# Five of the 47 expert tiles move from the main pipeline into a conditional block at the end of the program

## The chip, the cores and the metric

The kernel runs on one core of one Trainium2 chip. The metric is device microseconds of one execution. Beside it there is one profiled execution, with a trace of every engine: PE (matrix multiply; its weight loads are listed apart as PEld), DVE (vector), ACT (scalar activation), POOL (general purpose) and SP (issues most transfers).

## The reference, cut to what matters

Two layers on x of shape (4, 512, 256), all in float32. Layer 0 adds a linear attention with a running sum and a top-32 "gene" block. Layer 1 adds a running-sum mixer with a gated feed-forward part, and a mixture of experts:

```
xn = layernorm(x)                                  # 2048 tokens of 256
scores = softmax(xn @ gate_w.T)                    # 16 experts
topk_w, topk_idx = top_k(scores, 2)
gu = einsum('th,ehj->etj', xn, w_gate_up)          # 256 -> 352, per expert
h  = silu(gu[..., :176]) * gu[..., 176:]
y  = einsum('eti,eih,te->th', h, w_down, combine)  # only the two chosen experts count
y += swiglu(xn @ shared_gate_up) @ shared_down
```

Each token goes to two of 16 experts, which makes 2048 · 2 = 4096 rows of experts' work. How they are spread over the experts depends on the data.

## The kernel before, in words

**Main phases.** Tokens are worked on in 16 blocks of 128 (`NTT`). First layer 0 (`layer0`) and the layer-1 mixer (`mix`) run batch by batch, with the dense part of layer 1 (`dense`: shared expert and gated feed-forward, 88 steps of one chunk each) woven in between as filler for PE. `together` weaves generators by their weights.

**Routing.** `route` (L460 to L539) counts the tokens of each expert, rounds each count up to tiles of 128 rows and sums them up: `upto` holds the running number of tiles, so that its last element is the number of tiles that the routing needs. `offs` holds, for each of the `NTL` = 47 tiles, the offset of its expert's weights; 47 is the most that 4096 rows over 16 experts can need (32 full tiles and 15 more that are begun). `slot` and `cpair` give, for each token and choice, its row and its weight.

**Rows by way of DRAM.** `xrows` and `yrows` are arrays of 47 · 128 rows of 256 in DRAM. Early in the program one transfer (L173) fills `xrows` with zeros. `scatter` (L541) writes each token's row twice to `xrows` with 32 indirect transfers from POOL's queue, again beside dense steps. L682 to L793 are the experts' stage. It works in pairs of tiles: `fetch` (L707) loads two tiles of `xrows`; `turn_in` (L714) transposes them on PE, copies them to SBUF on ACT, and loads the pair's two offsets into PE registers; `up_tile` (L735) multiplies by the expert's gate and up weights, in the SBUF tile `wex` that holds all 16 experts, and makes silu on ACT and the product on DVE; `turn_hidden` (L751) transposes again; `down_pair` (L756) multiplies by the down weights, and the result goes to `yrows` on SP's queue. 47 tiles are 23 pairs and a single one, and `experts` (L774) runs 26 steps in which three pairs are in flight.

**The end.** Behind the experts come the last dense steps, with 32 indirect gathers (L806, `ys` from `yrows`, POOL's queue), 32 weighted adds on DVE (L817) and the stores of the output (L821, L826). The whole of `yrows` has to be written before the first gather starts.

**Order.** The order on each engine follows from the order in which the program issues its steps and from a scheduler that sets independent instructions among each other; on each engine the instructions then run in order. Transfers marked `paced` wait for the last dense matmul issued before them.

Of the kernel before, what the change touches and what calls it, by code (L numbers as in the profile page):

```python
# [11 lines left out]
F32 = mybir.dt.float32  # L12
AF = mybir.ActivationFunctionType
ALU = mybir.AluOpType
AX = mybir.AxisListType

P = 128
B, L, D = 4, 512, 256
NT = L // P
NH = D // P  # L20
# [3 lines left out]
NE, NI = 16, 176  # L24
EI = NE * NI
SI = 2 * NI
EW = NH * 2 * NI + 2 * D
NTT = B * NT
NTL = 47
XG = 2  # L30
HB = 2 * P
QSCALE = 0.25
# [5 lines left out]
def run_all(steps):  # L38
    for _ in steps:
        pass  # L40


def together(*streams):

    live = [[iter(steps), n, 0] for steps, n in streams]
    while live:
        s = min(live, key=lambda s: s[2] / s[1])
        s[2] += 1
        if next(s[0], live) is live:
            live.remove(s)  # L50
# [3 lines left out]
def tile_two_layers(  # L54
# [23 lines left out]
    nc = tc.nc  # L78
    V, S, G, T = nc.vector, nc.scalar, nc.gpsimd, nc.tensor

    const = ctx.enter_context(tc.tile_pool(name="const", bufs=1))


    xs = const.tile([P, B, NT, D], F32, name="xs")
# [7 lines left out]
    def paced(inst):  # L92

        tc.add_manual_dep(
            inst,
            beat[-1],
            mybir.DependencyInfo(mybir.DependencyClass.Sync, mybir.DependencyReason.DATA),
            reason="transfers spread over the dense parts",
        )
        return inst  # L100
# [61 lines left out]
    cpair = const.tile([P, 2, NTT], F32, name="cpair")  # L162
    slot = const.tile([P, 2, NTT], mybir.dt.int32, name="slot")
    offs = const.tile([1, NTL], mybir.dt.int32, name="offs")
    chosen = const.tile([P, NTT, NE], F32, name="chosen")
    cwall = const.tile([P, NTT, NE], F32, name="cwall")
    xn1 = const.tile([P, B, NT, D], F32, name="xn1")
# [1 line left out]
    yrows = tc.dram_tile([NTL * P, D], F32, name="yrows")  # L169
    zero = wp.tile([P, D], F32, name="zero")  # L170
    G.memset(zero, 0.0)

    nc.sync.dma_start(  # L173
        xrows.rearrange("(j p) d -> p j d", p=P), zero[:, None, :].to_broadcast([P, NTL, D])
# [285 lines left out]
    def route():  # L460


        rt = routing.enter_context(tc.tile_pool(name="rt", bufs=1))
        ps_r = routing.enter_context(tc.tile_pool(name="ps_r", bufs=1, space=bass.MemoryType.PSUM))

        stri = rt.tile([P, P], F32, name="stri")
        G.memset(stri, 1.0)
        G.affine_select(
            out=stri, in_=stri, pattern=[[1, P]], compare_op=ALU.is_gt, fill=0.0, base=0, channel_multiplier=-1
        )  # L470
        allone = rt.tile([P, P], F32, name="allone")
        G.memset(allone, 1.0)
        kfull = rt.tile([P, NE, NTT], F32, name="kfull")
        G.iota(
            kfull, pattern=[[0, NE], [P, NTT]], base=0, channel_multiplier=0, allow_small_or_imprecise_dtypes=True
        )
        jnum = rt.tile([P, NTL, NE], F32, name="jnum")
        G.iota(
            jnum, pattern=[[1, NTL], [0, NE]], base=0, channel_multiplier=0, allow_small_or_imprecise_dtypes=True
        )  # L480
        first0 = rt.tile([P, NE, NTT], F32, name="first0")
        G.memset(first0, 1.0)
        G.memset(first0[:, :, 0:1], 0.0)
        pr = ps_r.tile([P, L], F32, name="pr")
        flat = chosen.rearrange("p t e -> p (t e)")
        T.matmul(pr[:, 0 : NTT * NE], stri, flat, start=True, stop=True)
        T.matmul(pr[:, NTT * NE : L], allone, flat, start=True, stop=True)
        cnt = rt.tile([P, NE, NTT], F32, name="cnt")
        V.tensor_copy(cnt, pr[:, NTT * NE : L].rearrange("p (t e) -> p e t", e=NE))
        inc = rt.tile([P, NE, NTT], F32, name="inc")  # L490
        V.tensor_tensor_scan(
            inc.rearrange("p e t -> p (e t)"),
            first0.rearrange("p e t -> p (e t)"),
            cnt.rearrange("p e t -> p (e t)"),
            0.0,
            ALU.mult,
            ALU.add,
        )
        yield

        more = rt.tile([P, NE, NTT], F32, name="more")
        V.tensor_tensor(more, inc[:, :, NTT - 1 : NTT].to_broadcast([P, NE, NTT]), kfull, ALU.is_gt)
        nt = rt.tile([P, NE], F32, name="nt")
        V.tensor_reduce(nt, more, AX.X, ALU.add)
        upto = rt.tile([P, NE], F32, name="upto")
        V.tensor_tensor_scan(upto, allone[:, 0:NE], nt, 0.0, ALU.mult, ALU.add)
        yield

        past = rt.tile([P, NTL, NE], F32, name="past")
        V.tensor_tensor(past, upto[:, None, :].to_broadcast([P, NTL, NE]), jnum, ALU.is_le)  # L510
        ex = rt.tile([P, NTL], F32, name="ex")
        V.tensor_reduce(ex, past, AX.X, ALU.add)
        V.tensor_scalar(offs, ex[0:1], float(NE - 1), float(EW), ALU.min, ALU.mult)
        yield

        V.tensor_tensor(upto, upto, nt, ALU.subtract)
        V.tensor_scalar(upto, upto, float(P), 1.0, ALU.mult, ALU.add)
        V.tensor_tensor(inc, inc, cnt, ALU.subtract)
        V.tensor_tensor(inc, inc, upto[:, :, None].to_broadcast([P, NE, NTT]), ALU.add)
        row = rt.tile([P, NTT, NE], F32, name="row")  # L520
        V.tensor_tensor(
            row,
            pr[:, 0 : NTT * NE].rearrange("p (t e) -> p t e", e=NE),
            inc.rearrange("p e t -> p t e"),
            ALU.add,
        )
        V.tensor_tensor(row, row, chosen, ALU.mult)
        yield
        two = rt.tile([P, 2, NTT], F32, name="two")
        V.tensor_reduce(two[:, 0], row, AX.X, ALU.max)  # L530
        V.tensor_reduce(two[:, 1], row, AX.X, ALU.add)
        V.tensor_tensor(two[:, 1], two[:, 1], two[:, 0], ALU.subtract)
        V.tensor_scalar(slot, two, -1.0, None, ALU.add)
        for k in range(2):
            hit = rt.tile([P, NTT, NE], F32, name="hit")
            V.tensor_tensor(hit, row, two[:, k, :, None].to_broadcast([P, NTT, NE]), ALU.is_equal)
            V.tensor_tensor(hit, hit, cwall, ALU.mult)
            V.tensor_reduce(cpair[:, k], hit, AX.X, ALU.add)  # L538
        yield  # L539
# [23 lines left out]
    NC = len(chunks)  # L563
# [63 lines left out]
    def d(n):  # L627
        return islice(dd, n), n
# [4 lines left out]
    def m(b, i0, nt):  # L633
        return mix(b, i0, nt), 6 + nt
# [13 lines left out]
    weights = ctx.enter_context(ExitStack())  # L648
    we = weights.enter_context(tc.tile_pool(name="we", bufs=1, side="right"))


    wex = we.tile([P, NE * EW], F32, name="wex")
    wev = wex.rearrange("p (e w) -> p e w", w=EW)
    G.memset(wev[:, :, EW - D : EW], 0.0)

    def load_experts():
        wdv = w_down.rearrange("(e i) d -> i e d", i=NI)
        for e in range(0, NE, 4):
            es = slice(e, e + 4)
            for h in range(NH):  # L660
                paced(
                    nc.sync.dma_start(
                        wev[:, es, h * 2 * NI : (h + 1) * 2 * NI],
                        w_gate_up[es, h * P : (h + 1) * P, :].rearrange("e p j -> p e j"),
                    ).ins
                )
                yield
            paced(nc.sync.dma_start(wev[:, es, EW - 2 * D : EW - D], wdv[0:P, es]).ins)
            yield
            paced(nc.sync.dma_start(wev[0 : NI - P, es, EW - D : EW], wdv[P:NI, es]).ins)  # L670
            yield

    together(m(3, 0, 4), d(NC), (load_experts(), 17))
    mixing.close()
    routing = ctx.enter_context(ExitStack())
    together((route(), 8), d(5))
# [2 lines left out]

    run_all(islice(dd, 2 * NC - 19))  # L680

    wx = ctx.enter_context(tc.tile_pool(name="wx", bufs=2))  # L682
    hbs = []
    for k in range(2):
        hb = wx.tile([P, XG, 2 * P], F32, name=f"hb{k}", bufs=1)
# [2 lines left out]
    ps_u = ctx.enter_context(tc.tile_pool(name="ps_u", bufs=2, space=bass.MemoryType.PSUM))  # L688
    ps_x = ctx.enter_context(tc.tile_pool(name="ps_x", bufs=1, space=bass.MemoryType.PSUM))
    marks = []  # L690
    NP2 = (NTL + XG - 1) // XG
    pairs = {}

    def width(p):
        return min(XG, NTL - p * XG)

    def turned(src, m, name):

# [75 lines left out]
    def experts():  # L774

        for p in range(2):
            fetch(p)
        for s in range(NP2 + 2):
            if s + 2 < NP2:
                fetch(s + 2)  # L780
            if 0 <= s - 1 < NP2:
                up_tile(s - 1, 0)
            if s < NP2:
                turn_in(s)
            if 0 <= s - 1 < NP2:
                up_tile(s - 1, 1)
            if s - 2 >= 0:
                down_pair(s - 2)
            if 0 <= s - 1 < NP2:
                turn_hidden(s - 1)  # L790
            yield

    together((experts(), NP2 + 2))  # L793
    weights.close()

    back = ctx.enter_context(tc.tile_pool(name="back", bufs=1, side="right"))
    ys = back.tile([P, 2 * NTT, D], F32, name="ys")
    asked = 0  # L800
    added = 0
# [22 lines left out]
    assert asked == added == 2 * NTT  # L824
    for i in (NT - 2, NT - 1):
        nc.sync.dma_start(out[B - 1, i * P : (i + 1) * P], xs[:, B - 1, i])  # L826


# [47 lines left out]
```

## Time and profile before

| what | value |
|---|---|
| median of 3 runs | 586.94 us (586.6 to 588.18) |
| the profiled execution's own time | 591.42 us |
| its span in the trace | 589.7 us |
| mean granted PE clock | 0.975 |
| PE busy | 539.4 us (91%) |
| DVE, ACT, POOL busy | 373.1, 232.6, 173.9 us |
| the experts' stage, about 400 to 523 us | PE busy 122.04 of 123 us |

The span runs from the first to the last record of the trace; the execution's own time lies 1.7 us above it. The profiled execution took 4.5 us longer than the median of the runs. A row of the groups gives line, engine, operation, output and input tiles, count, then busy time and mean duration in ns, then the idle time ahead of them and what ended it. A row of the timeline begins with start and length in microseconds. One float32 matmul of the program appears as two passes in the trace, so a tile's two up matmuls are four rows.

### The profile page before, as it was taken

The numbers are of one execution on the slowest core, as the hardware profiler recorded it, in microseconds if no ns is written. First come the engines' busy times: TensorE is split into PE (matmuls) and PEld (weight loads), VectorE is DVE, ScalarE is ACT, GpSimd is POOL, SyncE is SP. The second block draws the span as 40 slices with busy tenths as digits, with TensorE's granted clock in tenths as the row PEclk, the third lists the DMA queues.
The fourth block names the chain that finished last, engine by engine and source line by source line (L and its number), as shares of the span: only waits on it lengthen the run. The fifth ranks groups of instructions, "written<-read, shape, count | busy, mean of one in ns | idle before, by whom it ended". The sixth has DMA issues, their size and how long they took to land.

```text
span 589.7 us, 7350 instructions
## 1 busy us (share of the span) xinstructions
PE 539.4 (91%) x2384; PEld 393.0 (67%) x2384; DVE 373.1 (63%) x992; ACT 232.6 (39%) x528; POOL 173.9 (29%) x214
## 2 busy tenths in 40 slices
PE   3557989989999999999999999969999999999987
PEld 1334656558565685656877778857777777788876
DVE  3979999997896797967943785322222222235563
ACT  1453746653555625556265311103333333321111
POOL 1234232353221432224440326661000000006651
PEclk9788999999999999999999999989999999999999
DMA  4993000000000000000075602224233333114441
GB/s 159 375 377 140 1 1 1 2 0 1 1 1 0 1 1 1 1 1 1 1 236 170 182 2 80 91 86 136 90 108 107 108 108 98 55 63 125 126 133 46
DMA packets 38453, 47.39 MB, mean 80 GB/s; under 512 B 4016, under 2 KB 34960, under 8 KB 38160
## 3 DMA queue, kind: packets, MB, share of 16 engines
q1 hardware_dynamic: 35344, 38.53, 20.0%
q0 software_dynamic: 3072, 8.39, 4.6%
q8 instruction: 20, 0.33, 0.2%
q14 instruction: 17, 0.14, 0.1%
HBM read 28.30 MB, written 18.61 MB: 80 GB/s over the span
## 4 chain that ended last, share of the span: by engine, by line
PE 61%; DVE 21%; ACT 6%; POOL 4%; issue 3%; DMA 2%; SPq 0%; another core or an unknown queue 0%; POOLq 0%; ACTq 0%; DVEq 0%
PE gu L576 16%; PE pu L740 9%; PE acc L596 9%; PE py L761 7%; PE pm L384 5%; DVE rep L302 4%; DVE top L301 4%; PE pt L703 3%; POOL xrows L544 3%; PE pm L244 3%; PE pm L289 2%; PE pm L221 2%; PE pm L339 2%; DVE sums L430 2%; DVE sums L421 1%
## 5 line engine op out<-in xcount | busy, mean ns | idle before, releaser
L576 PE MATMUL gu<-yT,wugt 128*128 128x256 f32 x512 | 127.5, 385 | 0.0
L576 PEld LDWEIGHTS gu<-yT,wugt 128*128 128x128 f32 x512 | 96.0, 192 | 19.5 <-issue 7.2
L580 ACT ACTIVATE th<-gu 128x256 f32<-128x256 f32 (+1 forms) x88 | 33.0, 382 | 133.4 <-PE gu L576 85.9
L806 POOL DMA_INDIRECT ys<-yrows,slot x32 | 30.7, 961 | 145.4 <-PE gu L576 130.1
L596 PE MATMUL acc<-wot,hid 128*128 128x256 f32 x256 | 67.4, 386 | 5.9 <-DVE hid L584 5.5
L582 DVE SCALAR_TENSOR_TENSOR th<-th,gu 128x256 f32<-128x256 f32 (+1 forms) x88 | 36.1, 412 | 55.0 <-ACT th L580 46.3
L740 PE MATMUL pu<-wex,xgT 128*128 x188 | 63.8, 461 | 0.8 <-DMA xg<-xrows 0.8
L587 POOL TENSOR_TENSOR hid<-hid,th 128x256 f32<-128x256 f32 (+1 forms) x44 | 34.3, 782 | 101.1 <-ACT hid L586 97.8
L596 PEld LDWEIGHTS acc<-wot,hid 128*128 128x128 f32 x256 | 48.4, 192 | 15.5 <-DVE hid L584 5.9
L244 PE MATMUL pm<-xnT,wqkv 128*128 128x512 f32 (+1 forms) x120 | 46.7, 529 | 4.1 <-ACT lg L293 1.8
L576 PE MATMUL gu<-xn1T,sgu 128*128 128x256 f32 (+1 forms) x192 | 47.3, 382 | 1.4 <-ACT hid L586 1.3
L749 DVE TENSOR_TENSOR hb<-pu,hb 128x176 f32<-128x176 f32 x47 | 16.1, 342 | 51.0 <-ACT hb L748 51.0
L384 PE MATMUL pm<-w,xn1T 128*128 128x512 f32 (+1 forms) x128 | 45.7, 501 | 0.0
L761 PE MATMUL py<-wex,hgT 128*128 x188 | 44.5, 379 | 0.0
L761 PEld LDWEIGHTS py<-wex,hgT 128*128 128x128 f32 x188 | 35.6, 190 | 8.6 <-issue 0.2
L576 PEld LDWEIGHTS gu<-xn1T,sgu 128*128 128x128 f32 (+1 forms) x192 | 33.8, 181 | 9.5 <-ACT hid L586 2.6
L740 PEld LDWEIGHTS pu<-wex,xgT 128*128 128x128 f32 x188 | 32.0, 190 | 11.0 <-ACT xgT L717 1.0
L384 PEld LDWEIGHTS pm<-w,xn1T 128*128 128x128 f32 x128 | 24.6, 193 | 21.4 <-issue 17.9
L244 PEld LDWEIGHTS pm<-xnT,wqkv 128*128 128x128 f32 x120 | 23.8, 202 | 22.0 <-issue 13.2
L753 DVE COPY hgT<-pt 128x512 f32<-128x512 f32 (+1 forms) x24 | 16.3, 681 | 34.2 <-PE pt L703 34.2
L544 POOL DMA_INDIRECT xrows<-xn,slot x32 | 31.0, 969 | 23.8 <-DVE cpair L538 9.9
L301 DVE MAX8 top<-rep 128x8 f32<-128x512 f32 x48 | 32.9, 686 | 0.4
(162 smaller groups left out, 881.5 us busy)
## 6 DMA issues: line engine op xcount, KB each, us to landing
xrows<-zero SPq DMA_DIRECT2D x1, 6016.0 KB, 22.6
xg<-xrows SPq DMA_DIRECT2D x23, 256.0 KB, 2.7
yrows<-yg SPq DMA_DIRECT2D x23, 256.0 KB, 2.1
wex<-in_w_gate_up_dram SPq DMA_DIRECT2D x8, 704.0 KB, 4.8
xs<-in_x_dram SPq DMA_DIRECT2D x4, 512.0 KB, 7.7
wugt<-in_wug_dram SPq DMA_DIRECT2D x1, 2048.0 KB, 12.3
wex<-in_w_down_dram SPq DMA_DIRECT2D x4, 512.0 KB
out_dram<-xs SPq DMA_DIRECT2D x7, 256.0 KB, 2.7
```

Source lines behind the costliest of these rows:

```text
L244: T.matmul(pm, wqkv[:, h, c * P : (c + 1) * P], xnT[:, h, 0:W], start=(h == 0), stop=(h == NH - 1),)
L301: V.max(tp[:, 8 * r : 8 * r + 8], src)
L384: T.matmul(o[:, 0:n], xnT[:, h, i * P : (i + 1) * P], w1[:, h, at : at + n], start=(h == 0), stop=(h == NH - 1),)
L544: sc = G.indirect_dma_start(out=xrows, out_offset=bass.IndirectOffsetOnAxis(ap=slot[:, k, i : i + 1], axis=0), in_=xn1[:, i // NT, i % NT] ...
L576: T.matmul(gu[0:m, k], w[:, h, at : at + m], ins[which][:, h], start=(h == 0), stop=(h == NH - 1))
L580: S.activation(th[0:m], gu[0:m, 0], AF.Tanh, scale=0.5)
L582: V.scalar_tensor_tensor(th[0:m], th[0:m], 1.0, gu[0:m, 0], ALU.add, ALU.mult)
L587: G.tensor_tensor(hid[0:m], hid[0:m], th[0:m], ALU.mult)
L596: mm = T.matmul(acc[:, t], hid[0:m, t * P : (t + 1) * P], dw[0:m, dc], start=(n == 0 and t == 0), stop=(n == NC - 1), skip_group_check=True,)
L740: T.matmul(pg[:, 0 : 2 * NI], xT[:, i, h], wex[:, bass.ds(at[i] + h * 2 * NI, 2 * NI)], start=(h == 0), stop=(h == NH - 1),)
L761: mm = T.matmul(py[:, i * D : (i + 1) * D], hT[:, i, h], wex[:, bass.ds(at[i] + EW - (2 - h) * D, D)], start=(h == 0), stop=(h == 1),)
L806: G.indirect_dma_start(out=ys[:, asked], out_offset=None, in_=yrows, in_offset=bass.IndirectOffsetOnAxis(ap=slot[:, k, n : n + 1], axis=0) ...
```

## The change

A new constant `NTU` = 42. The experts' stage works on the first 42 tiles, that is 21 full pairs, in every execution. The routing also keeps its count of tiles, as the integer `need`. The five last tiles of `yrows` are filled with zeros by one more transfer early in the program, ahead of the one for `xrows`. At the program's end every engine loads `need` into a register and compares it with 42; only if it is larger, `rest()` runs: it loads the experts' weights again, fills the first 42 tiles of `yrows` with zeros, works on tiles 42 to 46 one after the other, gathers all 32 blocks again, adds them to the output that still lies in SBUF, and stores the whole output once more. The loading of the weights becomes a function (`experts_in`) that both places call; where it stood before, it issues the same transfers in the same order. Two pools are closed before the branch, so that `rest()` has room.

```diff
 NTL = 47
+NTU = 42
...
+    need = const.tile([1, 1], mybir.dt.int32, name="need")
...
+    nc.sync.dma_start(
+        yrows[NTU * P :].rearrange("(j p) d -> p j d", p=P),
+        zero[:, None, :].to_broadcast([P, NTL - NTU, D]),
+    )
+
     nc.sync.dma_start(
         xrows.rearrange("(j p) d -> p j d", p=P), zero[:, None, :].to_broadcast([P, NTL, D])
     )
...
         V.tensor_scalar(offs, ex[0:1], float(NE - 1), float(EW), ALU.min, ALU.mult)
+        V.tensor_copy(need, upto[0:1, NE - 1 : NE])
         yield
...
-    NP2 = (NTL + XG - 1) // XG
+    NP2 = (NTU + XG - 1) // XG
...
     def width(p):
-        return min(XG, NTL - p * XG)
+        return min(XG, NTU - p * XG)
...
+    def rest():
+        with tc.tile_pool(name="late", bufs=1, side="right") as late:
+            wlate, transfers = experts_in(late)
+            run_all(transfers)
+            blank = late.tile([P, D], F32, name="blank")
+            G.memset(blank, 0.0)
+            nc.sync.dma_start(
+                yrows[0 : NTU * P].rearrange("(j p) d -> p j d", p=P),
+                blank[:, None, :].to_broadcast([P, NTU, D]),
+            )
+            for j in range(NTU, NTL):
+                rows = slice(j * P, (j + 1) * P)
+                xg = late.tile([P, D], F32, name="xg")
+                nc.sync.dma_start(xg, xrows[rows])
...
+                yg = late.tile([P, D], F32, name="yg")
+                S.copy(yg, py[:, 0:D])
+                nc.sync.dma_start(yrows[rows], yg)
+            for n in range(NTT):
+                here = xs[:, n // NT, n % NT]
+                for k in range(2):
+                    y = late.tile([P, D], F32, name="y", bufs=2)
+                    G.indirect_dma_start(
+                        out=y,
+                        out_offset=None,
+                        in_=yrows,
+                        in_offset=bass.IndirectOffsetOnAxis(ap=slot[:, k, n : n + 1], axis=0),
+                    )
+                    V.scalar_tensor_tensor(here, y, cpair[:, k, n : n + 1], here, ALU.mult, ALU.add)
+                nc.sync.dma_start(out[n // NT, n % NT * P : (n % NT + 1) * P], here)
...
+    late_rows.close()
+    held.close()
+    count = nc.values_load(need, min_val=0, max_val=NTL)
+    with tc.If(count > NTU):
+        rest()
```

More of the change, by code (lines that the diff above doesn't have):

```diff
@@ L649, in tile_two_layers, with experts_in, transfers @@
     we = weights.enter_context(tc.tile_pool(name="we", bufs=1, side="right"))
[L652 to L662, printed above, removed]
+    def experts_in(pool):
+        wex = pool.tile([P, NE * EW], F32, name="wex")
+        wev = wex.rearrange("p (e w) -> p e w", w=EW)
+        G.memset(wev[:, :, EW - D : EW], 0.0)
+        def transfers():
+            wdv = w_down.rearrange("(e i) d -> i e d", i=NI)
+            for e in range(0, NE, 4):
+                es = slice(e, e + 4)
+                for h in range(NH):
+                    yield nc.sync.dma_start(
                         wev[:, es, h * 2 * NI : (h + 1) * 2 * NI],
@@ L665, in load_experts @@
                     ).ins
[L666 to L673, printed above, removed]
+                yield nc.sync.dma_start(wev[:, es, EW - 2 * D : EW - D], wdv[0:P, es]).ins
+                yield nc.sync.dma_start(wev[0 : NI - P, es, EW - D : EW], wdv[P:NI, es]).ins
+        return wex, transfers()
+    wex, incoming = experts_in(we)
+    together(m(3, 0, 4), d(NC), (map(paced, incoming), 17))
     mixing.close()
@@ L680, in tile_two_layers @@
     run_all(islice(dd, 2 * NC - 19))
-    wx = ctx.enter_context(tc.tile_pool(name="wx", bufs=2))
+    held = ctx.enter_context(ExitStack())
+    wx = held.enter_context(tc.tile_pool(name="wx", bufs=2))
     hbs = []
@@ L791, in experts @@
             yield
+    def rest():
[12 more added lines that the diff above has]
+                nc.sync.dma_start(xg, xrows[rows])
+                pt = ps_x.tile([P, L], F32, name="pt")
+                for h in range(NH):
+                    T.transpose(pt[:, h * P : (h + 1) * P], xg[:, h * P : (h + 1) * P], ident)
+                xT = late.tile([P, NH, P], F32, name="xT")
+                S.copy(xT.rearrange("p h t -> p (h t)"), pt[:, 0:D])
+                at = nc.values_load(
+                    offs[0:1, j : j + 1],
+                    engines=[mybir.EngineType.PE],
+                    min_val=0,
+                    max_val=(NE - 1) * EW,
+                    skip_runtime_bounds_check_because="the expert's number is clamped where it is worked out",
+                )
+                pg = ps_u.tile([P, L], F32, name="pu")
+                for h in range(NH):
+                    T.matmul(
+                        pg[:, 0 : 2 * NI],
+                        xT[:, h],
+                        wlate[:, bass.ds(at + h * 2 * NI, 2 * NI)],
+                        start=(h == 0),
+                        stop=(h == NH - 1),
+                    )
+                hb = late.tile([P, 2 * P], F32, name="hb")
+                V.memset(hb[:, NI : 2 * P], 0.0)
+                S.activation(hb[:, 0:NI], pg[:, 0:NI], AF.Silu)
+                V.tensor_tensor(hb[:, 0:NI], pg[:, NI : 2 * NI], hb[:, 0:NI], ALU.mult)
+                pt = ps_x.tile([P, L], F32, name="pt")
+                for h in range(NH):
+                    T.transpose(pt[:, h * P : (h + 1) * P], hb[:, h * P : (h + 1) * P], ident)
+                hT = late.tile([P, NH, P], F32, name="hT")
+                S.copy(hT.rearrange("p h t -> p (h t)"), pt[:, 0:D])
+                py = ps_x.tile([P, L], F32, name="py")
+                for h in range(NH):
+                    T.matmul(
+                        py[:, 0:D],
+                        hT[:, h],
+                        wlate[:, bass.ds(at + EW - (2 - h) * D, D)],
+                        start=(h == 0),
+                        stop=(h == NH - 1),
+                    )
+                yg = late.tile([P, D], F32, name="yg")
[10 more added lines that the diff above has]
+                        in_offset=bass.IndirectOffsetOnAxis(ap=slot[:, k, n : n + 1], axis=0),
+                    )
+                    V.scalar_tensor_tensor(here, y, cpair[:, k, n : n + 1], here, ALU.mult, ALU.add)
+                nc.sync.dma_start(out[n // NT, n % NT * P : (n % NT + 1) * P], here)
@@ L793, in tile_two_layers @@
     together((experts(), NP2 + 2))
     weights.close()
-    back = ctx.enter_context(tc.tile_pool(name="back", bufs=1, side="right"))
+    late_rows = ctx.enter_context(ExitStack())
+    back = late_rows.enter_context(tc.tile_pool(name="back", bufs=1, side="right"))
     ys = back.tile([P, 2 * NTT, D], F32, name="ys")
```

## The prediction

> **What bounds the kernel now.** I read the page first, then the busy time by stretches, then PE's timeline inside the experts' stage, then the end of the timeline. The lines of the page that matter:
>
> ```profile
> span 589.7 us, 7350 instructions
> ...
> L740 PE MATMUL pu<-wex,xgT 128*128 x188 | 63.8, 461 | 0.8 <-DMA xg<-xrows 0.8
> ...
> L761 PE MATMUL py<-wex,hgT 128*128 x188 | 44.5, 379 | 0.0
> ...
> xrows<-zero SPq DMA_DIRECT2D x1, 6016.0 KB, 22.6
> ```
>
> The up and down matmuls of the experts occur 188 times each, four passes for each of 47 tiles, and ahead of them PE stood idle 0.8 us in all. The stretch of the experts' stage (its length, then busy time of PE, PEld, DVE, ACT, POOL, then clock, DMA share, GB/s):
>
> ```profile
> 400.00:523.00 123.00, 122.04 (x585) 93.61 (x584) 34.53 (x76) 44.01 (x97) 0.96 (x1) 1.00 0.32 100
> ```
>
> PE is busy 122.04 of 123 us, DVE and ACT about a third, the transfers a third, the clock full. Busy PE need not mean PE at its limit, so I look at the rhythm: starts in PE's timeline, one full pass, then the odd last tile's parts.
>
> ```profile
> 508.66 1.89 PE L761 MATMUL py<-wex,hgT 128*128 x8
> 510.38 0.60 PE L703 MATMUL pt<-ident,hb 128*128 128x128 f32 x4
> 510.82 1.35 PE L740 MATMUL pu<-wex,xgT 128*128 x4
> 512.00 0.60 PE L703 MATMUL pt<-ident,xg 128*128 128x128 f32 x4
> 512.44 1.35 PE L740 MATMUL pu<-wex,xgT 128*128 x4
> 513.63 1.89 PE L761 MATMUL py<-wex,hgT 128*128 x8
> ...
> 516.98 0.38 PE L703 MATMUL pt<-ident,xg 128*128 128x128 f32 x2
> 517.20 1.35 PE L740 MATMUL pu<-wex,xgT 128*128 x4
> ...
> 523.46 0.38 PE L703 MATMUL pt<-ident,hb 128*128 128x128 f32 x2
> 523.67 1.03 PE L576 MATMUL gu<-xn1T,sgu 128*128 128x256 f32 x4
> 524.54 1.03 PE L761 MATMUL py<-wex,hgT 128*128 x4
> 525.40 1.03 PE L576 MATMUL gu<-xn1T,sgu 128*128 128x256 f32 x4
> ```
>
> A pass takes 513.63 − 508.66 = 4.97 us, every group starts when the one before it is issued, and no row names an idle time. The stage is a chain on PE, and so is what follows: from 525.40 the dense groups start right behind each other. Work taken out here moves the end. The end itself:
>
> ```profile
> 585.54 0.69 DVE L607 TENSOR_TENSOR xs<-acc,xs 128x512 f32<-128x512 f32 x1 [1.29 <-PE acc L596]
> 586.26 0.82 SPq L826 DMA_DIRECT2D out_dram<-xs  x2
> ```
>
> The last matmuls release one add, that two stores, and 2.6 us after their issue (587.08) the span ends at 589.7; the median landing of these stores is 1.7 us, so about 0.9 us are left for the closing waits of SP and the end.
>
> [...]
>
> **Is the branch entered?** This decides the sign. Worked out from the reference's formula on its inputs, the experts get 129, 510, 333, 99, 170, 915, 429, 63, 39, 194, 51, 30, 73, 632, 410 and 19 rows. Rounded up to 128 these are 2+4+3+1+2+8+4+1+1+2+1+1+1+5+4+1 = 41 tiles. Rounding could move a row from one expert to another; 43 would need two experts to step over a multiple of 128, and the nearest below one (510 and 632) need 3 and 9 rows more. So 42 is enough, by one tile, and the branch is passed.
>
> **The change part by part**, against the profiled execution (591.42 us, span 589.7):
>
> 1. Five tiles less. Two full passes: 2 × 4.97 = 9.94 us. The single tile, from starts: transposes in 517.20 − 516.98 = 0.22; up 1.19 (as 513.63 − 512.44); hidden transposes 523.67 − 523.46 = 0.21; down 525.40 − 524.54 = 0.86; together 2.48. Sum −12.42 us on PE. Five times two PE offset loads, five silus, five products and the copies of 2.5 pairs go too (ACT, DVE); they lie under PE. Their 256 KB fetches and stores go from SP's queue, which waits for others in this stage.
> 2. The last pair is now full. In the built order PE runs its hidden transposes, four dense passes (0.87 us) and then the down matmuls. DVE's copy of a full pair takes 0.69 us (681 ns a row, against 0.42 for a single tile); with the starts seen one pass earlier (transposes 520.11, copy 520.74 to 521.43, and 0.24 us from copy to matmul as at 524.30 to 524.54) the down matmuls could start 1.56 us after the transposes, PE reaches them after 0.43 + 0.87 = 1.30. Cost +0.26 us.
> 3. `need`: one DVE copy of one element, in the routing ahead of the scatter. Small DVE rows there take 0.15 to 0.17 us; started behind each other about 0.1. The scatter's 32 transfers on POOL (each 0.97 and a gap of 0.30) follow `slot`, and the chain of waits runs in part through them: +0.1 us, 0 at least. A dense product moves two reductions earlier on DVE; that is only better for PE.
> 4. The zero fill of five tiles, 640 KB, goes ahead of the one for `xrows` on SP's queue. At 6016 KB / 22.6 us = 266 KB per us it takes 2.4 us, plus an issue of about 1 us. It stands behind all loads of inputs (last issue before 28.37 us), and what it delays, the fill of `xrows`, lands near 53 instead of 51 us; its first user is the scatter at 356 us. Cost 0. Without that cover it would be 3.4 us.
> 5. SP's register load of `need` stands, in the built order, behind the weights' loads (issued by 335 us) and ahead of the first `xg` fetch. It waits for a DVE result of about 350 us; the fetches queued behind it wait for the scatter until 402.66 us. Cost 0.
> 6. The end. PE, ACT and POOL come to their load and branch with their work done, before the last add. DVE issues the last add at 585.54, [...] while the stores land near 588.8. SP holds its register already; it jumps, waits there for the stores, then has some five more short semaphore steps than before and a branch, at 0.05 to 0.1 us each: +0.3 to 0.5 us. [...] The nearest thing in the trace: near 393.5 us ACT and POOL come out of waits with the releaser "remote", 9.53 and 2.79 us, POOL's usual gap being 0.30[...]. Of such 2.5 us on DVE about 1.2 would be covered by the landing, on SP some 1.7. So +0.3 at the least, about +3 at the most, and I take +0.9. A gain is excluded: nothing at the end is removed.
>
> Sum: −12.42 + 0.26 + 0.1 + 0.9 = −11.16 us. The profiled execution would be 580.3 us. The runs' median is 4.5 us lower; in the profile PE stood 5.46 us at 394.83 behind the waits just named, which I suspect for most of that difference. As none of the removed work is there, I apply the same difference to the median: 586.94 − 11.16 = 575.8 us.
>
> **The rivals.** *A dear end:* four engines' jumps or loads are not covered and cost 3 to 6 us. For it: "remote" waits occur; against it: only SP and DVE are late enough to matter. 586.94 − 12.1 + 4.5 = 579.4 us. *The gain is partly given back behind the experts:* the gathers wait for the last `yrows` store and DVE's adds wait for gathers; once (561.92 us) PE stood 1.82 us behind a DVE add that was queued so. The last store is now 256 KB (2.1 us to land) instead of 128 KB (2.3), so its distance to the dense steps stays; if such a stall came two times more, 579 us as well, once more 577.6. *The branch is entered* (the slower side): it decides as soon as `need` is over 42. Weights again, 8 × 704 + 4 × 512 + 4 × 192 = 8448 KB at 266 KB per us, 32 us; 42 tiles of zeros, 5376 KB, 20 us; five tiles in a row at some 7 us (a landing 2.7, and the PE, ACT and DVE rows), 35 us; 32 gathers with two buffers, about 2 us each, 64 us. Some 150 us: about 725 us. *The change doesn't do what it says* — PE waits for `xg` as soon as it has less to do — is excluded by the rhythm: a pass keeps its own 4.97 us.
>
> **How the numbers follow.** Forecast as worked out 0.78 (its own range 574.8 to 577.6, the end's +0.3 to +2.7); dear end 0.10; given back behind the experts 0.06; branch entered 0.03; 0.03 for a larger gain (stalls of PE vanish, 573). Range 573.8 to 579.5: it leaves out the branch, half of the dear end and of the larger gain. 0.3% of 586.94 us is 1.8 us, about what these runs can tell from no change; all cases but the branch lie beyond it on the fast side. Faster 0.95, same 0.02 (a dear end of twice the size), slower 0.03.
>
> **What would show it.** Right: 21 passes of 4.97 us; 168 rows each of L749 and L770 up and down matmuls; no second load of weights; the last add about 12 us earlier than 585.54; from the last stores' issue to the end of the span not over 3.5 us. Step 2 is wrong if PE idles over 0.5 us ahead of the last down group; step 4, if anything before 60 us but the two fills has moved; step 6, if the tail is 2 us longer or the span ends on DVE. I am wrong altogether if rows of `rest()` appear.

## The result, and the profile after

| | before | after |
|---|---|---|
| median of the runs side by side | 587.12 us (586.6 to 588.18, 4 runs) | 576.85 us (576.04 to 577.69, 4 runs) |
| ratio | 1 | 0.9828, 95% interval 0.9811 to 0.9844 |
| profiled execution, its span | 591.42 us, 589.7 us | 576.85 us, 575.1 us |

The change makes the kernel faster by 10.27 us, median against median; the ratio's interval is 9.2 to 11.1 us of 587.12. The forecast was 575.8 us, in a range of 573.8 to 579.5. The profiled execution of before lies 4.3 us above the median of its runs, that of after on it, so the spans (14.6 us apart) overstate the change; the experiments show with which wait that comes.

The page of the kernel after has these rows for the experts' matmuls:

```profile
span 575.1 us, 7191 instructions
...
L749 PE MATMUL pu<-wex,xgT 128*128 x168 | 58.3, 470 | 0.8 <-DMA xg<-xrows 0.8
...
L770 PE MATMUL py<-wex,hgT 128*128 x168 | 39.8, 379 | 0.0
```

There are 168 passes instead of 188 in each, four for each of 42 tiles: the main part has 42 tiles, and no row of `rest()` occurs. The up rows are 470 ns in the mean instead of 461, of which more below. The middle of the experts' stage by busy time (stretch, length, then PE, PEld, DVE, ACT, POOL, clock, DMA share, GB/s), and the two zero fills among the transfers (KB each, us to landing):

```profile
407.00:508.00 101.00, 100.81 (x484) 76.72 (x483) 27.81 (x61) 35.84 (x80) 0.00 (x0) 1.00 0.30 92
```
```profile
xrows<-zero SPq DMA_DIRECT2D x1, 6016.0 KB, 23.3
...
yrows<-zero SPq DMA_DIRECT2D x1, 640.0 KB, 8.5
```

PE is as full as before. The fill of `xrows`, now behind the added one, takes 0.7 us longer from issue to landing and is issued 0.7 us later; it lands at 52.3 us instead of 50.9, some 300 us ahead of its first use.

PE's timeline at the end of the experts' stage (start, length, then the instruction), the down groups that begin and end one full pass, and then the last pass:

```profile
496.55 1.89 PE L770 MATMUL py<-wex,hgT 128*128 x8
...
501.52 1.89 PE L770 MATMUL py<-wex,hgT 128*128 x8
503.24 0.60 PE L712 MATMUL pt<-ident,hb 128*128 128x128 f32 x4
503.68 2.53 PE L749 MATMUL pu<-wex,xgT 128*128 x8
506.05 1.89 PE L770 MATMUL py<-wex,hgT 128*128 x8
507.78 0.60 PE L712 MATMUL pt<-ident,hb 128*128 128x128 f32 x4
508.21 1.03 PE L584 MATMUL gu<-xn1T,sgu 128*128 128x256 f32 x4
509.25 1.96 PE L770 MATMUL py<-wex,hgT 128*128 x8
511.05 1.03 PE L584 MATMUL gu<-xn1T,sgu 128*128 128x256 f32 x4
```

The pass is 501.52 − 496.55 = 4.97 us as before. There are now only full pairs; the last pass turns no new rows, and the last down group starts 1.47 us after its transposes (507.78 to 509.25), 0.17 us later than the transposes and the dense passes between (0.43 + 0.87) would let it.

The end, from the timeline; then, from the records of single lines, the steps of the sequencers (count, shortest/median/longest in ns, first and last start):

```profile
569.70 0.69 DVE L615 TENSOR_TENSOR xs<-acc,xs 128x512 f32<-128x512 f32 x1 [1.29 <-PE acc L604]
570.42 1.31 SPq L905 DMA_DIRECT2D out_dram<-xs  x2
```
```profile
L911 DVEq TENSOR_LOAD <-need x1: 543/543/543, 569.7 to 569.7; - x1
```
```profile
L912 SPq EVENT_SEMAPHORE  x8: 17/17/17, 572.3 to 573.4; - x8
...
L912 DVEq COMPARE_BRANCH  x1: 76/76/76, 570.3 to 570.3; - x1
L912 DVEq EVENT_SEMAPHORE  x1: 21/21/21, 570.9 to 570.9; - x1
L912 SPq COMPARE_BRANCH  x1: 45/45/45, 571.8 to 571.8; - x1
```
```profile
L959 SPq EVENT_SEMAPHORE  x14: 17/28/28, 573.5 to 575.1; - x14
```

The branch is there and is passed over. From the start of the last add to the end of the span it is now 575.1 − 569.70 = 5.40 us; before, 589.7 − 585.54 = 4.16. DVE is through with load, compare and jump at 570.9, long before the end. SP compares at 571.8 and has its first step behind the jump at 572.3. There it goes through eight steps, in which it waits for the last stores, until 573.4, and it has all 14 closing steps still ahead of it.

And PE in front of the experts' stage:

```profile
401.66 1.09 PE L712 MATMUL pt<-ident,xg 128*128 128x128 f32 x4 [3.81 <-DMA xg<-xrows]
403.50 2.71 PE L749 MATMUL pu<-wex,xgT 128*128 x4 [0.75 <-DMA xg<-xrows]
```

PE waits 3.81 us for the first rows of the experts, and the first up group then takes 2.71 us instead of the 1.35 of a later one. The profile of before has neither; there PE had waited in the middle of the scatter and came to the first expert tile only at 406.00, without a wait:

```profile
394.83 2.07 PE L596 MATMUL acc<-wot,hid 128*128 128x256 f32 x4 [5.46 <-DVE hid L584]
...
406.00 0.60 PE L703 MATMUL pt<-ident,xg 128*128 128x128 f32 x4
```

### The profile page after: what moved, and what is told of

It reads as the page before. It is cut to its first block, busy times and chain, and to the rows that moved or that the text cites. A ratio compares the mean times of both kernels' runs of the same rounds, so it can differ in the third digit from the quotient of the medians.

```text
span 575.1 us, 7191 instructions
## 1 busy us (share of the span) xinstructions
PE 527.4 (92%) x2324; PEld 383.5 (67%) x2324; DVE 370.3 (64%) x985; ACT 228.4 (40%) x517; POOL 173.6 (30%) x214
## 4 chain that ended last, share of the span: by engine, by line
PE 54%; DVE 22%; POOL 8%; ACT 7%; issue 4%; DMA 4%; SPq 0%; POOLq 0%; ACTq 0%; DVEq 0%
PE gu L584 12%; PE pu L749 9%; PE acc L604 7%; PE py L770 6%; PE pm L391 5%; DVE rep L309 4%; DVE top L308 4%; POOL xrows L552 3%; PE pt L712 3%; POOL ys L885 3%; PE pm L251 3%; PE pm L296 2%; PE pm L228 2%; PE pm L346 2%; DVE sums L437 2%
## 5 line engine op out<-in xcount | busy, mean ns | idle before, releaser
L584 PE MATMUL gu<-yT,wugt 128*128 128x256 f32 x512 | 126.0, 381 | 0.0
L604 PE MATMUL acc<-wot,hid 128*128 128x256 f32 x256 | 66.2, 381 | 0.4
L749 PE MATMUL pu<-wex,xgT 128*128 x168 | 58.3, 470 | 0.8 <-DMA xg<-xrows 0.8
L758 DVE TENSOR_TENSOR hb<-pu,hb 128x176 f32<-128x176 f32 x42 | 14.3, 341 | 51.9 <-ACT hb L757 51.9
L770 PE MATMUL py<-wex,hgT 128*128 x168 | 39.8, 379 | 0.0
L770 PEld LDWEIGHTS py<-wex,hgT 128*128 128x128 f32 x168 | 31.8, 190 | 7.9 <-issue 0.4
L749 PEld LDWEIGHTS pu<-wex,xgT 128*128 128x128 f32 x168 | 29.4, 195 | 10.5 <-ACT xgT L726 1.2
L762 DVE COPY hgT<-pt 128x512 f32<-128x512 f32 x21 | 14.5, 691 | 30.0 <-PE pt L712 30.0
L296 PE MATMUL pm<-wct,xnT 128*128 128x512 f32 x64 | 33.4, 659 | 0.3 <-ACT xnT L244 0.2
```

The costliest lines, as they stand in the source:

```text
L296: T.matmul(pl, xnT[:, h, i * P : (i + 1) * P], wct[:, h], start=(h == 0), stop=(h == NH - 1))
L584: T.matmul(gu[0:m, k], w[:, h, at : at + m], ins[which][:, h], start=(h == 0), stop=(h == NH - 1))
L604: mm = T.matmul(acc[:, t], hid[0:m, t * P : (t + 1) * P], dw[0:m, dc], start=(n == 0 and t == 0), stop=(n == NC - 1), skip_group_check=True,)
L749: T.matmul(pg[:, 0 : 2 * NI], xT[:, i, h], wex[:, bass.ds(at[i] + h * 2 * NI, 2 * NI)], start=(h == 0), stop=(h == NH - 1),)
L770: mm = T.matmul(py[:, i * D : (i + 1) * D], hT[:, i, h], wex[:, bass.ds(at[i] + EW - (2 - h) * D, D)], start=(h == 0), stop=(h == 1),)
```

## The experiments

Theory A is the prediction's: 12.4 us of matrix work go, and the block at the end gives 1 to 2 us back. Rival B: the block costs nothing, and five tiles are worth less. Rival C: the count or the zero fill costs what is missing of the gain. All ratios are to the kernel before, run side by side.

### The changed kernel again, without the block, and with one tile less

The first is the changed kernel unaltered.

> The changed kernel once more, as the measure for the runs beside it: 0.983 of the kernel before, 576.9 us. Both theories the same.

Measured 577.11 us, ratio 0.9831 (0.9816 to 0.9846). Without the block:

```diff
-    count = nc.values_load(need, min_val=0, max_val=NTL)
-    with tc.If(count > NTU):
-        rest()
```

> Leaves the conditional block out (register loads, compares, body, and the semaphore steps that stand for the body); 42 tiles, the count and the zero fill stay. It would be short of rows for a routing that needs more than 42 tiles. Theory A (five tiles are worth 12.4 us of matrix work, and the block at the end costs what the gain lacks, some 1.9 us): 575.0 us, and the span ends 4.2 us after the start of the last add instead of 5.4. Rival B (the block costs nothing that shows, 0.3 us or less; the five tiles themselves are worth only some 10.5 us): 576.6 us. Rival C (the gain's missing part is the fill or the count in front of the scatter): 576.6 us too, told from B by the other runs.

Measured 575.13 us, ratio 0.9792 (0.9773 to 0.9811): 2.0 us less than the changed kernel beside it by the medians. This is 12.2 us under the kernel before (11.1 to 13.3), with fill and count in place. So neither rival B nor rival C explains what the gain lacks; up to about 1 us for count and fill lies inside the interval. In the profile the span ends at 572.6 and the last add starts at 568.63, so the end takes 3.97 us instead of 5.40.

```diff
-NTU = 42
+NTU = 41
```

> 41 tiles in the main part (20 pairs and a single one), the block entered at more than 41. If the routing needs 41 tiles, as worked out, the block is passed over, and the single tile less saves the second half of a pass: theory A 2.4 us less than with 42, 574.4 us; rival B (a tile is worth only 10.5/5 = 2.1 us) 574.8 us. If the routing needs 42, the block is entered and the time is over 700 us.

Measured 573.89 us, ratio 0.9776 (0.9761 to 0.9791). The block is not entered, so the routing needs at most 41 tiles. The single tile is worth 3.2 us by the medians (each ratio is known to about 0.9 us); in the profiles, from the first expert tile to the last add, it takes 565.05 − 399.80 = 165.25 us, against 567.25 − 399.74 = 167.51 and 569.70 − 401.66 = 168.04 in the two profiles with 42 tiles, that is 2.3 to 2.8 us for the tile, around the 2.48 us of the prediction.

### The block alone on the kernel before

```diff
-    NP2 = (NTU + XG - 1) // XG
+    NP2 = (NTL + XG - 1) // XG
...
-        return min(XG, NTU - p * XG)
+        return min(XG, NTL - p * XG)
...
-    with tc.If(count > NTU):
+    with tc.If(count > NTL):
```

> All 47 tiles in the main part as before, with the count, the fill and the same conditional block at the end, entered at more than 47, so never. Theory A: the block and its preparations alone cost 1.5 to 2.2 us over the kernel before, 588.9 us (ratio 1.003). Rival B: 587.3 us (ratio 1.000).

Measured 587.82 us, ratio 1.0017 (1.0008 to 1.0027), between the two forecasts. Its profile holds no compare, and a load of the count on SP alone: the count's upper bound was 47, so the condition "over 47" was known to be false. What remained at the end were the block's semaphore steps, which stand for the signals of the skipped body, and with them alone the end takes 587.0 − 582.10 = 4.90 us. With a bound of 48 the compare stays:

```diff
-    count = nc.values_load(need, min_val=0, max_val=NTL)
-    with tc.If(count > NTU):
+    count = nc.values_load(need, min_val=0, max_val=NTL + 1)
+    with tc.If(count > NTL):
```

> As the run with all 47 tiles in the main part and the block at the end, but with a bound on the count that keeps the compare in the program; in the earlier run the condition was known to be false from the bounds, and the loads and compares were dropped, though the block's semaphore steps stayed. Theory A (the block costs what it adds behind the last stores): 5.4 to 5.6 us from the start of the last add to the end of the span, 1.4 us over the kernel before, 588.6 us (ratio 1.0024). Rival B (loads and jumps are covered; only the semaphore steps count): 4.9 us and 0.7 us over before, as without them (ratio 1.001).

Measured 589.45 us, ratio 1.0044 (1.0029 to 1.0059): the block, with the count and the fill that this run also holds, costs 1.7 to 3.5 us of time. In the profile the end takes 587.8 − 582.04 = 5.76 us, 1.6 more than before. This profile is also the cleanest partner for the changed kernel, as PE waits the same 3.8 to 3.9 us in front of the experts in both: from the first expert tile to the last add it takes 582.04 − 401.54 = 180.50 us with 47 tiles and 168.04 with 42, a difference of 12.46 us. Theory A holds for both of its terms: the tiles are worth what was said, and the block costs over 1 us.

### Why the end is longer: a short body

The body is replaced by one that works over the last output again, so it stays behind the last stores:

```diff
     def rest():
-        with tc.tile_pool(name="late", bufs=1, side="right") as late:
-            wlate, transfers = experts_in(late)
-...
+        for i in (NT - 2, NT - 1):
+            V.tensor_scalar(xs[:, B - 1, i], xs[:, B - 1, i], 1.0, None, ALU.mult)
+            nc.sync.dma_start(out[B - 1, i * P : (i + 1) * P], xs[:, B - 1, i])
```

In the changed kernel the last two stores land 2.3 us after their issue in the median, in the kernel before 1.7. Theory A1 puts that down to the jump over the long body, theory A2 to any jump or to the loads.

> 42 tiles and a branch behind the last add as in the changed kernel, but the block's body is two small vector instructions and two stores, so it would not help a routing that needs more than 42 tiles. The jump is over a few instructions, and there are two semaphore steps on SP instead of eight. Theory A1 (the stores land late [...]): the last stores land after 1.7 to 1.8 us instead of 2.3, 17 instead of 20 packets on the second instruction queue, 4.4 us from the last add's start to the end, 575.6 us. Rival A2 (any taken jump does it, or the loads): landing stays 2.3 us, about 5.2 us to the end, 576.6 us.

Measured 574.94 us, ratio 0.9806 (0.9791 to 0.9821). The landing of the last two stores, from the records of their line, is first that of the changed kernel, then of the short body, then of the kernel before (shortest/median/longest in us):

```profile
DMA to landing us min/median/max: 2.1/2.3/2.5
```
```profile
DMA to landing us min/median/max: 1.7/1.8/1.8
```
```profile
DMA to landing us min/median/max: 1.7/1.7/1.7
```

With the short body the stores land as before and the end takes 572.3 − 568.29 = 4.01 us, as long as without the block (3.97), though loads, compares and jumps are there. In time this run lies between the changed kernel (0.9831) and the one without the block (0.9792), and its interval overlaps both. So in the profiles the price hangs on the jump over a long body, as in theory A1, and not on loads or any jump, as in A2. It has two parts.

The last store lands later. From the start of the last add to the last landing it takes 3.6 to 3.8 us in all eight profiles in which the long body is jumped over. It takes 2.9 us in the six others: both profiles of the kernel before, the ones without the block, without its compare and with the short body, and the one below in which the block is entered. In that last one, loads and compares run ahead of the same long body, but it is not jumped over.

And SP's steps stand behind the landing. In the second profile of the changed kernel SP sees the last landing at 571.0 and comes to its first DRAIN record at 571.9, with fourteen steps between, two in the block and twelve behind it; in the kernel before there are five, from 588.5 to 588.9. With the short body most of SP's steps lie under the landing, as its block waits for other stores.

Why the stores land later is not shown. The second queue of instructions carries 17 packets in the kernel before, without the compare and with the short body, 16 without the block, and 20 wherever the long block has its compare. In each of the eight profiles with the long jump, two packets of 8 KB of this queue start between the stores' issue and the last landing, in the changed kernel at 571.83 and 572.84, with the stores issued from 570.42 and landed at 573.29. In the six others none does. SP's first step behind the jump comes 0.5 us after its compare there, and 0.2 us with the short body. So the two packets, the long jump and the late landing go together in all fourteen profiles; whether the packets delay the stores, or something else that comes with a long jump does, no run separates.

### The idle time in front of the experts

```diff
-    run_all(islice(dd, 2 * NC - 19))
+    run_all(islice(dd, 2 * NC - 18))
```

> The changed kernel with one dense step more ahead of the experts' stage and one less behind it. In the profile after, PE stands 3.8 us in front of the first expert tile, because the scatter's last rows and the first fetch land later than the dense steps end. If that idle time is real in every run, the step (2.59 us) fits into it: 574.4 us, idle 1.2 us. If it belongs to the profiled execution alone, or the tail is bound by the gathers once it is shorter: no change, 577 us.

Measured 572.33 us, ratio 0.9768 (0.9752 to 0.9783): by the ratios 3.7 us less than the changed kernel in the set of runs before this one (0.9831 to 0.9768 of 586), more than the 2.59 us of the step. Its profile shows why:

```profile
400.87 0.63 PE L712 MATMUL pt<-ident,xg 128*128 128x128 f32 x4 [1.24 <-DMA xg<-xrows]
402.25 1.45 PE L749 MATMUL pu<-wex,xgT 128*128 x4 [0.75 <-ACT xgT L726]
```

PE now waits 1.24 us instead of 3.81, and the first up group takes 1.45 us instead of 2.71. In the changed kernel the granted clock is 0.50 from 402 to 406 us, after 3.81 us of waiting; here, after 1.24 us, the second up group at 403.97 already takes the 1.35 us of a later one. In the seven profiles in which PE waits 3.63 to 4.05 us there, the first up group takes 2.67 to 2.72 us; where between 1.24 and 3.63 us this begins was not measured. The idle time thus costs its own length and the slow groups behind it, 1.26 us in this group alone.

### The block entered

```diff
-NTU = 42
+NTU = 40
```

> 40 tiles in the main part, and the block entered at more than 40. If the routing needs 41, as worked out and as the run with 41 tiles allows, the block is entered: theory A with the prediction's estimate of the body, about 150 us and two more tiles: 720 us. If the routing needs 40 or fewer: 572 us.

Measured 737.23 us, ratio 1.2572 (1.2548 to 1.2597). With the run at 41 this fixes the count: the routing needs 41 tiles. The slower rival is real, and the branch decides at the count at which the prediction said it would. Pieces of the chain of waits (start, length, what):

```profile
588.77 21.04 DMA xg<-xrows
611.40 2.70 PE pu L830 x4
...
619.31 2.73 PE pu L830 x4
...
665.18 1.70 DMA yrows<-yg
668.95 2.69 DMA y<-yrows,slot
```

The weights take the 24 us from the last stores at 564.96 to 588.77 (32 estimated). The zero fill then holds the first rows up for 21 us (20 estimated), a tile takes 619.31 − 611.40 = 7.9 us (7 estimated; PE's clock is at 0.50 here), and the gathers take the 70 us from 665 to the end of the span at 735.4 (64 estimated). For seven tiles in place of five the estimate of 150 us becomes some 165, and from the last stores to the end it is 170. That these sums lie so close is in part luck, as the weights were put too high and the rest too low. The expectation of 720 us was 17 us too low; it left out most of what the two more tiles take.

### Both gains together, and the kernel before once more

```diff
-NTU = 42
+NTU = 41
...
-    run_all(islice(dd, 2 * NC - 19))
+    run_all(islice(dd, 2 * NC - 18))
```

> 41 tiles in the main part and one dense step more ahead of the experts' stage, with the block of the changed kernel at the end, so right for every routing. If the two gains add up (one tile 2.5 us and what the step brought, 3.8 us): 570.5 to 571 us, ratio 0.972. If the tail behind the experts becomes bound by the gathers: 572 us or more.

> The kernel before, looked at once more. The prediction suspects the 5.46 us for which PE stood at 394.83 us of belonging to that one execution. If so: no such wait in this profile, PE stands about 3.9 us in front of the first expert tile instead, as in the other profiles, the first expert tile starts near 401.5 us instead of 406, and the profiled time is near 587 us. If it belongs to the kernel: the wait is there again, 591 us.

Measured 577.59 us, ratio 0.9773 (0.975 to 0.9797), so the expected 570.5 to 571 us did not come, and for the kernel before 590.59 us, in a set of runs in which its median was 590.67. The profile of before shows the wait again at nearly the same place:

```profile
393.98 2.07 PE L596 MATMUL acc<-wot,hid 128*128 128x256 f32 x4 [4.71 <-DVE hid L584]
```

ACT came out of an 8.81 us wait there whose releaser is "remote", which means that the profile does not tell it, and POOL out of one of 2.72. The wait was in no profile of the first two sets of experiments, and it does not belong to one execution alone, as one side of the expectation had it: it comes in whole sets of runs, and where it comes, the kernel before takes 590 to 591.5 us instead of 586 to 587. The 4.5 us by which the profiled execution of before exceeded its runs are of the same size and come with the same wait. Each of the four sets ran on another chip (0, 10, 6 and 14 in the record; the wait came on the last two), so it may as well go with the chip. The last two runs, side by side in such a set:

> 41 tiles and the dense step more, beside the same with 42 tiles. In the earlier runs with 41 tiles and the step, PE stood 3.97 us in the middle of the scatter, as in the profile of the kernel before, and the kernel before took 590.7 us there instead of 586 to 587. If that wait is absent here: ratio 0.972 to 0.973, and one tile (2.5 us) faster than the run beside it. If it is present: ratio 0.977 again, still 2.5 us faster than the run beside it.

> The changed kernel with the dense step more, beside 41 tiles. If the wait in the middle of the scatter is absent: ratio 0.977, PE stands 1.2 us in front of the first expert tile. If it is present: the step finds no idle time to fill, ratio 0.981 to 0.983.

Measured 578.22 us, ratio 0.9779 (0.976 to 0.9797), for 41 tiles, and 578.87 us, ratio 0.9807 (0.9784 to 0.983), for 42, beside 591.46 us for the kernel before. The wait was present in both, 5.41 us at 395.44 and 5.63 us at 380.44, and where it is, PE reaches the first expert tile late enough to find its rows there, so the step more finds no idle time there to fill. The single tile is worth 1.7 us by the ratios here; from the first expert tile to the last add the two profiles take 571.51 − 409.66 = 161.85 and 571.32 − 406.82 = 164.50 us, 2.65 us apart. Both versions were faster than the kernel before in every set in which they ran; whether 41 tiles with the step beat 42 with it also where the wait is absent was not measured.

## Why the prediction was right, point by point

**What bounds the kernel.** Right: taking out 20 + 20 matmul passes and their transposes shortened the way to the last add by their full length, at an unchanged 4.97 us a pass. The sign "last add about 12 us earlier than 585.54" holds only against the run with 47 tiles and the block; in the first profile after it is 15.8 us earlier, as the profile of before holds the wait in the scatter.

**Is the branch entered.** Right: 41 tiles, fixed by the runs at 41 and at 40.

**Step 1, five tiles, −12.42 us, and step 2, the full last pair, +0.26.** Together −12.16; measured −12.46 between the two profiles in which the compare is there, and −12.2 us (−11.1 to −13.3) in time without the block. The last pair shows as 0.17 us of wait and a down group after which the next starts 1.80 us later instead of 1.73, 0.24 in sum.

**Steps 3 to 5, count, fill and SP's load, +0.1 us.** Right within about 1 us: the run without the block holds them and is as fast as the tiles alone explain. The fill took 8.5 us to land, behind the last loads of inputs, and nothing waits for it. The sign against step 4, that anything before 60 us moves, can't be read: PE's steps there start up to 0.4 us earlier or later than in the profile of before (9.32 against 9.64 us, 53.06 against 52.72), while two profiles of the changed kernel are themselves 2.1 us apart at the scatter's first transfer (356.9 and 354.8 us). The load of the count on SP took 0.47 us at 350 us.

**Step 6, the end, +0.9 us.** Right in kind, undersized, and the working put the cost in the wrong place. The two ends it gave, 0.3 and 3, hold the measured +1.24 us of the first profile and +1.6 of the block alone on the kernel before, but that is in part luck, as what I had as the risk, late load and jump on DVE, is covered: DVE is done at 570.9 of 575.1. What load, compare and jump would take on DVE was my estimate and rested on no trace, as the profile of before holds no such branch; the load took 0.54 us there and the compare 0.08. What costs is the landing of the last store, 2.5 us after its issue instead of 1.8, which the sum had as unchanged, and SP's steps behind it, fourteen in 0.9 us instead of five in 0.4, where I counted some five more than before. The sign of not over 3.5 us from the last stores' issue to the end was met in the first profile (3.4 us, from the end of the issue) only because the issue itself took longer there; in the second it is 4.0.

**The sum.** −12.46 + 1.24 to 1.6 gives −10.9 to −11.2 us; the medians say −10.27, the ratio's interval −9.2 to −11.1. By time the block costs about 2.3 us (from 0.9831 to 0.9792) or 2.6 (1.7 to 3.5), by the profiles' ends 1.4 to 1.6. Up to a microsecond between the two is not accounted for by any stretch read here, and lies at the edge of the intervals; it stays open. So the forecast came within about 1 us of the result because the large term, the tiles, was right; the small one, the end, was not.

**The rivals.** A dear end (3 to 6 us) did not come; the block's interval reaches to 3.5. Nothing was given back behind the experts: PE's wait behind a DVE add there is 0.33 us in the profile after and 0.34 with 47 tiles and the block, so the 1.82 of the first profile did not come with the tiles. The entered block costs what was estimated, with errors in its parts that cancel.

**The difference of profile and runs.** I carried it over unchanged and suspected the 5.46 us wait; it comes with sets of runs, as shown. ACT and POOL do not wait for a transfer of instructions, as far as the trace shows: in the profile of before no packet of an instruction queue is on its way between 379.3 and 419.0 us, while ACT waits from 383.95 to 393.48, and in the four later profiles with such a wait none is during it either. What it is stays open.

## What to carry to other kernels

If PE is the bound and the data need less than the worst case, moving the rare part into a block at the end is worth the passes it saves; here some 12.4 us for a price of about 2. Work out the count on the actual inputs first, for it sets the sign: the block entered with seven tiles costs 170 us. And look at how long a skipped body is and what lies behind the last stores: a short body cost nothing that showed in the profile, a long one some 0.7 us of landing and 0.6 us of closing steps.

## What was not expected of the hardware

- Where a long body is jumped over just before, the last two stores land 1.9 to 2.1 and, where a second landing is recorded, 2.5 to 2.6 us after their issue instead of 1.7 and 1.8, and two packets of the second instruction queue are on their way meanwhile. Where the body is short, or long and entered, neither is so.
- A condition that the declared bound of the value makes false takes loads and compares out of the program, but leaves the block's semaphore steps: 0.74 us at the end.
- In some sets of runs ACT and POOL wait up to 9.5 and 2.8 us for "remote" in the middle of the scatter, and PE with them for 4 to 5.6 us, at 374 to 395 us; in these sets the indirect transfers of the scatter, where a landing is recorded, land after 2.6 to 3.1 us in the median instead of 2.4 or 2.5. In the profile of before no packet of an instruction queue is on its way from 379.3 to 419.0 us, around the wait; the cause was not found.
